# A two-layer attention and expert kernel on one core: the stores of the scan's values, and the seam between the layers

## The chip, the core and the metric

The kernel runs on one core of one Trainium2 chip. The core has five engines which run side by side, each through its own list of instructions, in order: PE (TensorE: matrix products and transposes, with PEld for its weight loads), DVE (VectorE), ACT (ScalarE), POOL (GpSimd) and SP (SyncE, which here does nothing but issue transfers). Transfers (DMAs) run on 16 shared DMA engines; ScalarE and SyncE issue theirs to hardware queues, GpSimd to a software queue. Engines and transfers wait for each other through semaphores. In the profile, "ACTq", "SPq" or "POOLq" stands for an engine's transfer queue.

The metric is the device time of one execution, in microseconds (us). The time of a kernel is the median over several runs.

## What is computed

Two layers, each `x = x + attention(layernorm(x)) + experts(layernorm(x))`, on x of 8 batches x 512 tokens x 256 features, in 32-bit floats.

```python
x = L0_attn_x
xn = _layernorm(x, axis=-1)
x = x + _L0_attn_ref(xn, ...) + _L0_ffn_ref(xn, ...)
xn = _layernorm(x, axis=-1)
x = x + _L1_attn_ref(xn, ...) + _L1_ffn_ref(xn, ...)
```

Layer 0's attention is a recurrence over the tokens, forwards and backwards. Tokens are mixed with their neighbours in five ways; products of these give r, k, v, a gate g and a decay w; then for each of 16 heads (16 x 16 states)

```python
def fwd_step(S, inp):
    rt, kt, vt, wt = inp
    S = jnp.exp(wt)[..., None] * S + kt[..., None] * vt[..., None, :]
...
y = (y_f + y_b).transpose(1, 0, 2, 3).reshape(B, T, D)
y = y * jax.nn.sigmoid(dx @ gate_w + gate_b)
yn = ((yg - mu) / jnp.sqrt(var + eps)).reshape(B, T, D) * ln_w + ln_b
return yn * g @ Wo
```

Layer 0's experts: 8 of them, each token goes to the best two. Layer 1's attention is a sum of two: a causal one whose keys and values come through a 64-wide latent, and one with a window of 64 tokens, both with 16 query heads over 4 key and value heads, with rotary positions and normalised queries and keys. Layer 1's experts: 16 small ones in 4 groups (4 per token, from the best two groups), and a shared one that every token passes.

## The kernel before

**Storage order.** Layer 0 runs batch after batch. The normalised tokens of all batches lie in eight tiles, held0 to held7, until they have been stored, and layer 1 uses these places again. Work tiles of layer 0 come from a pool `rw`: tiles with the same tag share a place, so a new one waits until the old one's readers are done.

**Who sets the order.** The program is written as coroutines. A class `Turns` goes round the running ones and lets each put out instructions up to its next `yield`; a second list, `behind`, gets its turn after the first. So the order of instructions on PE, VectorE, ScalarE and SyncE is that of the turns; GpSimd's alone is put in order by the scheduler. [...]

**One batch of layer 0**, in the code's names:
- `projections(b)` (lines 740 to 910), for the batch after the one being scanned. `mixed` multiplies on PE (L764, tile m), mixes on VectorE (L770) and lets GpSimd add the tokens with an accumulating transfer (L774). `values` computes v, copies it to the tile v (L828) and stores it to `vd` in memory (L830, from ScalarE's queue), then k. `decays` makes the decay, r and the tiles dq and dqs (L885 to L896) and the gate g (L906).
- `spread(b, c, vg)` (L912 to L919) loads `vd` back with 8 transfers of 64 KB from SyncE (L917), each value spread over partitions, into one of four kv tiles.
- `scans` (L926 to L982): 128 steps, 16 for each batch. A step is, on VectorE, a product (L943), two scans along the tokens (L952 forwards, L960 backwards) and a product (L965), about 7 us in all; PE sums the heads (L971, tile ys). The loads for a step are issued ahead.
- `ending(b, c, y, z, x)` (L984 to L1049), twice a batch: gate (L990), normalise (L994 to L1028), times g on GpSimd (L1030, tile z). After the second half, PE multiplies with the output weights (L1040, tile o), ScalarE copies the result to the tile x (L1045), GpSimd adds the layer's input with an accumulating transfer (L1046), and after eight turns SyncE stores x to `after` (L1049).
- beside it the experts (L594 to L682): for each of 39 chunks GpSimd gathers the weights (wgu and wdn, L582) and the tokens' rows (xs, L592) by indirect transfers; PE transposes and multiplies (g and u L630, y L670); ScalarE and VectorE make h (L654, L639); ys is copied (L679) and stored to `outs` (L680).

**The seam.** `begin()` (L1062 to L1093) runs late in layer 0. ScalarE issues loads of layer 1's first constants (cstr, rtw, cbias, L1069 to L1071) and, when the last value has been spread, of weights (gq, go, lqkv at L1088, the shared expert's w1 at L1092). It also starts layer 1's entry and routing for batch 0. `entry(b)` (L285 to L328) loads `after` (L290), gathers the two expert outputs of each token on GpSimd (L299, tile y0), accumulates them on VectorE (L310), normalises (statistics L236, root on GpSimd L229, L243), transposes on PE (L269) and copies to the tile xT (L324). `routing(b)` (L330 to L384) chooses the experts, on VectorE mostly.

Layer 1 then loads its remaining constants (cst1, gdown, gup, lo_w, L1116 to L1127). Its first instructions on batch 0 are the squares sq_g and the scaled tokens xg_g (L1189, L1191), the latent product lat_g (L1197), the products qkv (L1215, L1219), rotation and normalising (L1237 to L1264) and the transposes of queries qT_g (L269); beside them runs the shared expert (g and u L1427, h L1464 to L1472, y L1483). The entries and routings of batches 1 to 7 stand in the list behind (L1505 to L1510).

## Time and profile before

| what | value |
|---|---|
| median of 3 runs | 2606.01 us (2602.91 to 2608.89) |
| the profiled execution's own time | 2599.81 us |
| its span, first to last instruction | 2598.0 us |
| mean clock granted to PE, as a share of full speed | 0.942 |
| last batch's o in layer 0 ends / first xg_g of layer 1 starts | 1401.3 us / 1413.1 us |

The profiled execution is 1.8 us longer than its span, and 6.2 us below the median. Busy times by stretch, where the bounds of the first rows are the 17th, 33rd and so on of the scan's first products (L943), one batch each:

| stretch, us | length | PE busy | VectorE busy | granted clock |
|---|---|---|---|---|
| 284.8 to 449.0 | 164.2 | 144.6 | 141.6 | 0.95 |
| 449.0 to 601.6 | 152.6 | 141.7 | 142.7 | 0.97 |
| 601.6 to 755.9 | 154.3 | 144.9 | 143.0 | 0.96 |
| 755.9 to 920.6 | 164.7 | 145.5 | 141.8 | 0.96 |
| 920.6 to 1072.9 | 152.3 | 141.6 | 142.8 | 0.96 |
| 1072.9 to 1229.9 | 157.0 | 145.4 | 142.9 | 0.93 |
| 1229.9 to 1413.0 | 183.1 | 104.0 | 141.9 | 0.74 |
| 1413.0 to 1560.0 | 147.0 | 123.8 | 92.7 | 0.94 |

How the views are read. The page's second part cuts the span into 40 slices of 65 us and gives the busy tenths of each engine. In the view of waits a line has the engine, the waiting instruction, after the arrow what released it, and then the sum of the waits in us, their number and the longest. In the timeline a line has the start and the busy time in us, the engine, the code line, the operation, what it writes and reads, and in brackets the idle time just before it and what ended it.

### The profile page before, as it was taken

To read this page: it belongs to the slowest core of one execution; us is meant where nothing else is said; L and a number is where in the kernel's file an instruction comes from. 1 tells how busy PE (TensorE), PEld (TensorE's weight loads), DVE (VectorE), ACT (ScalarE), POOL (GpSimd) and SP (SyncE) were. 2 spreads that over 40 slices of the span, in tenths; PEclk is the share of its full clock that TensorE was granted. 3 is DMA by queue.
4 is the path that set the end of the run, shared out by engine and by line. 5 is a ranking of instruction groups with operands and counts; after the bars stand their busy time and mean duration, and the time that the engine had idled before them with its cause. 6 is when DMAs were issued, how large, how long until landed. Compare 5 with 4: busy or idle time off the path is not lost. (4 is left out here: it accounts for less than half of the span.)

```text
span 2598.0 us, 32354 instructions
## 1 busy us (share of the span) xinstructions
PE 2301.5 (89%) x11772; PEld 1369.8 (53%) x11772; DVE 2027.3 (78%) x2695; ACT 973.9 (37%) x1794; POOL 484.4 (19%) x424
## 2 busy tenths in 40 slices
PE   6688898989988899899925799999999999999998
PEld 4265555656655566555602444554555555555555
DVE  6699979999897998989984656686767667685566
ACT  1334224343322434224202244444444444445444
POOL 1123332233332322333111110010101010000000
PEclk9779999999999999999956899999999999999999
DMA  7546676776766767675543100020111101000000
GB/s 234 137 116 179 159 188 169 183 199 170 198 181 156 185 176 201 188 173 172 152 119 104 47 21 26 9 60 15 37 30 29 38 21 38 17 26 17 21 1 26
DMA packets 113885, 274.01 MB, mean 105 GB/s; under 512 B 25760, under 2 KB 51136, under 8 KB 108608
## 3 DMA queue, kind: packets, MB, share of 16 engines
q0 software_dynamic: 38448, 145.12, 21.3%
q1 hardware_dynamic: 66304, 109.13, 15.6%
q10 hardware_dynamic: 8976, 17.70, 2.0%
q8 instruction: 95, 1.56, 0.3%
q14 instruction: 62, 0.51, 0.1%
HBM read 215.22 MB, written 31.46 MB: 95 GB/s over the span
## 5 line engine op out<-in xcount | busy, mean ns | idle before, releaser
L670 PE MATMUL y<-wdn,h 128*128 128x256 f32 x936 | 271.5, 425 | 45.6 <-DVE h L639 38.3
L952 DVE TENSOR_TENSOR_SCAN kv<-dqs,kv 128x1024 f32<-128x1024 f32 x128 | 293.1, 2290 | 3.8
L960 DVE TENSOR_TENSOR_SCAN kv<-ds,kv 128x1024 f32<-128x1024 f32 x128 | 292.0, 2281 | 1.8
L670 PEld LDWEIGHTS y<-wdn,h 128*128 128x128 f32 x936 | 174.2, 203 | 165.2 <-issue 76.0
L630 PE MATMUL g<-xsT,wgu 128*128 128x256 f32 x936 | 227.5, 386 | 0.0
L1333 ACT ACTIVATE pt_g<-sc_g 128x512 f32<-128x512 f32 (+1 forms) x384 | 170.9, 533 | 148.7 <-PE sc_g L1325 140.9
L1483 PE MATMUL y<-w,h 128*128 128x256 f32 x768 | 202.9, 402 | 5.6 <-DVE h L1472 4.8
L630 PEld LDWEIGHTS g<-xsT,wgu 128*128 128x128 f32 x936 | 175.8, 192 | 53.5 <-issue 30.0
L1427 PE MATMUL g<-xT,w 128*128 128x512 f32 x384 | 192.4, 624 | 8.9 <-DVE h L1469 4.1
L630 PE MATMUL u<-xsT,wgu 128*128 128x256 f32 x780 | 196.5, 392 | 2.0 <-ACT h L654 2.0
L943 DVE TENSOR_TENSOR kv<-kv,k 128x1024 f32<-128x1024 f32 x128 | 159.3, 1244 | 45.1 <-DMA kv<-vd 45.0
L1427 PE MATMUL u<-xT,w 128*128 128x512 f32 x384 | 191.7, 621 | 1.8 <-DVE h L1469 0.9
L630 PEld LDWEIGHTS u<-xsT,wgu 128*128 128x128 f32 x780 | 147.2, 194 | 53.4 <-issue 17.3
L1483 PEld LDWEIGHTS y<-w,h 128*128 128x128 f32 x768 | 138.8, 193 | 62.6 <-issue 36.1
L965 DVE TENSOR_TENSOR kv<-kv,r 128x1024 f32<-128x1024 f32 x128 | 156.4, 1222 | 3.1
L971 PE MATMUL ys<-kv,cst 128*32 128x512 f32 x512 | 103.2, 659 | 60.8 <-DVE kv L965 60.8
L654 ACT ACTIVATE h<-g 128x512 f32<-128x512 f32 (+1 forms) x117 | 60.9, 525 | 234.2 <-PE g L630 222.8
L1333 ACT ACTIVATE pt_l<-sc_l 128x384 f32<-128x384 f32 (+1 forms) x256 | 98.2, 472 | 123.0 <-PE sc_l L1325 82.7
L592 POOL DMA_INDIRECT xs<-normed,whose x78 | 123.0, 1577 | 49.3 <-issue 18.0
L1470 DVE TENSOR_TENSOR h<-h,u 128x512 f32<-128x512 f32 x96 | 66.0, 687 | 76.2 <-PE u L1427 71.8
L1341 DVE TENSOR_TENSOR pt_l<-pt_l,cst 128x768 f32<-128x768 f32 (+1 forms) x128 | 108.0, 885 | 18.1 <-ACT pt_l L1333 18.1
L582 POOL DMA_INDIRECT wgu<-in_w_gu,wrow x39 | 66.4, 1703 | 287.4 <-PE u L630 285.7
(313 smaller groups left out, 3820.0 us busy)
## 6 DMA issues: line engine op xcount, KB each, us to landing
kv<-vd SPq DMA_DIRECT2D x1024, 64.0 KB
xf<-xnT POOLq DMA_DIRECT2D x40, 512.0 KB
cb<-cd SPq DMA_DIRECT2D x128, 128.0 KB
outs<-ys POOLq DMA_DIRECT2D x39, 256.0 KB
w<-in_w ACTq DMA_DIRECT2D x12, 384.0 KB
xn<-in_x SPq DMA_DIRECT2D x8, 512.0 KB
xnT<-xT ACTq DMA_DIRECT2D x16, 256.0 KB
normed<-xn SPq DMA_DIRECT2D x8, 512.0 KB
```

What stands on the lines that cost most here:

```text
L592: pool_e.indirect_dma_start(out=xs[:, n, :], out_offset=None, in_=normed, in_offset=bass.IndirectOffsetOnAxis(ap=whose[:, at : at + 1], ax ...
L630: pe.matmul(o, w[:, at + c * P : at + (c + 1) * P], xT[:, c, :], start=c == 0, stop=c == NC - 1,)
L670: pe.matmul(y[:, n, :], hs[j // 2][lo:, j % 2, n * P : (n + 1) * P], wd[lo:, j * D : (j + 1) * D], start=j == 0, stop=j == NJ0,)
L943: vec_e.tensor_tensor(kv, kv, bc(kc, 1, NV), ALU.mult)
L952: vec_e.tensor_tensor_scan(out=flat, data0=qc, data1=flat, initial=0.0, op0=ALU.mult, op1=ALU.add)
L960: vec_e.tensor_tensor_scan(out=flat[:, ::-1], data0=dc[:, ::-1], data1=flat[:, ::-1], initial=0.0, op0=ALU.mult, op1=ALU.add,)
L965: vec_e.tensor_tensor(kv, kv, bc(rc, 1, NV), ALU.mult)
L971: pe.matmul(y[r0 : r0 + 32, :], C["take"][:, 24 - 8 * at : 56 - 8 * at], kv[:, i, :], start=at == 0, stop=at == 3, skip_group_check=True,)
L1333: act_e.activation(pt[:, i, :end], scs[i][:, :end], AF.Exp, scale=0.25)
L1341: vec_e.tensor_tensor(pt[:, :, a0 : a0 + m], pt[:, :, a0 : a0 + m], bc(mask[:, :m], 1, 4), ALU.mult,)
L1427: pe.matmul(ps, w[:, k, c * P : (c + 1) * P], xT[:, c, :], start=c == 0, stop=c == NC - 1,)
L1483: pe.matmul(y[:, i, :], hs[k][:, (t + i) * P : (t + i + 1) * P], w1[j - 5 + k][:, 2, :], start=k == 0, stop=k == 5,)
```

## The change

Five things are changed.

1. The store of v to `vd` goes out from ScalarE's queue for the first batch alone, from GpSimd's for the other seven.
2. The tag "x" is gone. Two tiles of the routing of layer 0 (past, parts) and the tile x of batches 0 to 6 take the tag "dq" (one place); x is taken at the end of `ending`.
3. For the last batch, x is the tile held5. SyncE loads the layer's input into it ahead, and VectorE adds o to it straight from PSUM, in place of ScalarE's copy, GpSimd's accumulating load and the eight turns.
4. The constants cst1 are loaded in `begin()`, behind cstr, and gdown and gup behind lqkv.
5. `entry(1)` runs in layer 0, after the routing of batch 0; the list behind in layer 1 starts at batch 2. The routing of batch 1 stays in that list.

```diff
@@ two_layers
+    cst1 = const.tile([P, NCONST - last1], F32, name="cst1")
@@
-            past = tmp([P, NCH, E0], "past", "x")
+            past = tmp([P, NCH, E0], "past", "dq")
...
-            parts = rw.tile([P, 5, NTT], F32, tag="x", name="parts")
+            parts = rw.tile([P, 5, NTT], F32, tag="dq", name="parts")
@@ values
-                act_e.dma_start(vd.rearrange("(c p) t -> p c t", p=P), v)
+                (act_e if first else pool_e).dma_start(vd.rearrange("(c p) t -> p c t", p=P), v)
@@ scans
-                    x = rw.tile([P, NT, D], F32, tag="x", name=f"x_{b}")
...
-                        turns.add(ending(b, c, y, z, x))
+                        turns.add(ending(b, c, y, z))
@@ ending
             made.pop(b)
+            final = b + 1 == B
+            if final:
+                x = held(5, [P, NT, D], f"x_{b}")
+                nc.sync.dma_start(x, tokens(a["x"][b]))
+            else:
+                x = rw.tile([P, NT, D], F32, tag="dq", name=f"x_{b}")
             yield
...
-                act_e.copy(x[:, t : t + 2, :], ps)
-            pool_e.dma_start(x, tokens(a["x"][b]), accum_op=ALU.add)
-            for _ in range(8):
-                yield
+                if final:
+                    vec_e.tensor_tensor(x[:, t : t + 2, :], x[:, t : t + 2, :], ps, ALU.add)
+                else:
+                    act_e.copy(x[:, t : t + 2, :], ps)
+            if not final:
+                pool_e.dma_start(x, tokens(a["x"][b]), accum_op=ALU.add)
+                for _ in range(8):
+                    yield
             nc.sync.dma_start(tokens(after[b]), x)
@@ begin
             act_e.dma_start(cstr, a["cst"][:, first1:last1])
+            act_e.dma_start(cst1, a["cst"][:, last1:])
+            for n, (lo, hi) in _C.items():
+                if lo >= last1:
+                    C[n] = cst1[:, lo - last1 : hi - last1]
...
-            turns.add(then(entry(0), routing(0)))
+            turns.add(then(entry(0), routing(0), entry(1)))
...
-                ("lqkv", "l_wqkv", [P, NC, D + P]),
+                ("lqkv", "l_wqkv", [P, NC, D + P]), ("gdown", "g_kv_down", [P, NC, 64]),
+                ("gup", "g_up", [64, P]),
@@ layer 1
-        cst1 = keep.tile([P, NCONST - last1], F32, name="cst1")
-        act_e.dma_start(cst1, a["cst"][:, last1:])
...
-        gdown = keep.tile([P, NC, 64], F32, name="gdown")
-        act_e.dma_start(gdown, a["g_kv_down"])
-        gup = keep.tile([64, P], F32, name="gup")
-        act_e.dma_start(gup, a["g_up"])
+        gdown, gup = W["gdown"], W["gup"]
...
-                for b in range(1, B)
+                for b in range(2, B)
```

More of the change, by code (lines that the diff above doesn't have):

```diff
@@ L965, in scans, with sums @@
                 vec_e.tensor_tensor(kv, kv, bc(rc, 1, NV), ALU.mult)
-                def sums(b=b, c=c, vg=vg, kv=kv, y=y, z=z, x=x):
+                def sums(b=b, c=c, vg=vg, kv=kv, y=y, z=z):
                     for i in range(NV):
@@ L982, in scans, with ending @@
                 sums()
-        def ending(b, c, y, z, x):
+        def ending(b, c, y, z):
             sig, g = made[b]["sig"], made[b]["g"]
@@ L1114, in two_layers @@
         ps_o = l1.enter_context(tc.tile_pool(name="ps_o", bufs=1, space=PSUM))
-        cst1 = keep.tile([P, NCONST - last1], F32, name="cst1")
-        act_e.dma_start(cst1, a["cst"][:, last1:])
-        for n, (lo, hi) in _C.items():
-            if lo >= last1:
-                C[n] = cst1[:, lo - last1 : hi - last1]
         gq, go, lqkv = W["gq"], W["go"], W["lqkv"]
-        gdown = keep.tile([P, NC, 64], F32, name="gdown")
-        act_e.dma_start(gdown, a["g_kv_down"])
-        gup = keep.tile([64, P], F32, name="gup")
-        act_e.dma_start(gup, a["g_up"])
+        gdown, gup = W["gdown"], W["gup"]
         lo_w = keep.tile([P, NC, D], F32, name="lo_w")
```

## The prediction

> **What bounds the kernel now.** I read the page first: its busy shares and 40 slices, the waits of each engine's instructions, then the timeline of two places.

> ```profile
> PE 2301.5 (89%) x11772; PEld 1369.8 (53%) x11772; DVE 2027.3 (78%) x2695; ACT 973.9 (37%) x1794; POOL 484.4 (19%) x424
> ...
> PE   6688898989988899899925799999999999999998
> ...
> DVE  6699979999897998989984656686767667685566
> ...
> PEclk9779999999999999999956899999999999999999
> ```

> One slice is 65 us. Layer 0 ends near 1402 us (slice 21), layer 1 starts at 1413. From slice 25 PE is full, so layer 1 is PE's; in layer 0 PE and VectorE are both near 90%, in a fixed order with each other, and at slices 20 to 22 neither is: that is the junction, with PE's clock down.

> ```profile
> SPq L917 <- DMA vd<-v: 122.4, 8, 36.9
> ...
> SPq L917 <- DMA cstr<-in_cst: 11.9, 1, 11.9
> ...
> DVE kv L943 <- DMA kv<-vd: 45.0, 10, 9.3
> ...
> DVE xg_g L1191 <- DMA after<-x: 20.8, 1, 20.8
> PE lat_g L1197 <- DVE xg_g L1191: 11.5, 1, 11.5
> PE qT_g L269 <- DVE qn_g L1259: 7.6, 1, 7.6
> ```

> SyncE's queue, which loads the scan's values (L917), waits 8 times for a store `vd<-v`. One batch of layer 0 shows why that is odd:

> ```profile
> 352.75 0.37 ACTq L830 DMA_DIRECT2D vd<-v  x1
> 357.81 4.53 SPq L917 DMA_DIRECT2D kv<-vd  x9
> 362.25 1.23 DVE L943 TENSOR_TENSOR kv<-kv,k 128x1024 f32<-128x1024 f32 x1 [6.56 <-DMA kv<-vd]
> ```

> At 357.81 SyncE loads the scan's 8th step of a batch. It needs that batch's vd, stored 150 us before; yet it goes only when the next batch's vd, issued at 352.75 from ScalarE's queue, has landed. That is a wait for an order of completions among the hardware queues, not for data, and VectorE stands idle 6.56 us at L943. It comes once for each of the stores b = 1 to 7.

> **Part 1, the stores b >= 1 go to GpSimd's queue.** The stalls at L943 which follow a vd store are, at 200.47, 362.25, 670.21, 833.76 and 1143.77 us, 3.55, 6.56, 6.84, 6.59 and 8.94 us; at the other two stores (511.61, 983.17) nothing is left of it. Sum 32.5 us. The two last stalls of the row, 1.57 at 1310.69 and 9.31 at 1334.70, follow the constant loads in begin() (cstr and others), not vd; they stay. What one stall is worth depends on what comes next, since VectorE's lead lasts only until it waits for PE:
> - b = 1: nearly whole, 3.5 us.
> - b = 2: PE is busy through the stall, and VectorE's mixing (L770, at 368.65) waits for PE's m of 365.25. With the lead it would start at 366.5 and no earlier: about 1.8 us. b = 5 has the same order and numbers: 1.8 us.
> - b = 4: PE waits 2.33 us for L770 at 676.92 and then runs slowly, m in 2.73 us instead of 1.13 and u in 3.78 instead of 1.88. Without the stall the gate L990, at 686.53, would come at about 681.4: 5.1 us.
> - b = 7: L990 at 1160.54 would come at about 1152.8, as m was ready from 1143: 7.7 us.

> Sum 3.5 + 1.8 + 5.1 + 1.8 + 7.7 = 19.9, say 20 us. Check by batch periods: from scan step to scan step the batches last 164.2, 152.6, 154.3, 164.6, 152.3 and 157.0 us; the two without a stall are the short ones, and those with the stalls of b = 2, 4, 5 and 7 exceed 152.5 by 11.7, 1.8, 12.1 and 4.5. Their sum, 30, is near the stalls' 28.9, but batch by batch they don't match my leads, and PE's work in them is some 3 us larger (144.6 to 145.5 against 141.6), so I don't price by periods. Bounds: 0 if PE takes every lead, 32.5 if none is lost.

> Cost on GpSimd: the nearest row is its 512 KB accumulate (L1046), 1.29 to 1.45 us each, so 7 x 1.4 = 10 us on an engine that is 19% busy. Behind the stores stand gathers: for b = 2 the down weights, which were issued at 355.06 (they waited for PE y till 354.80) and are used at 373.63, 18.6 us later; for b = 1, 4, 7 one row gather of xs, used 27 us later; for b = 3 and 6 GpSimd is idle some 14 us there (504.12 to 518.46). Cost taken: 0; without that cover up to 10 us. The new true wait, the next batch's first load after its store, has some 75 us of slack, and SyncE's later loads stand behind it.

> The slow m and u belong to PE's clock: granted 0.58 at 676 to 683 us after a wait of 2.33, 0.72 at 207 to 213 after one of 2.41. [...]

> **Part 2, the junction.** Before, the last batch's tokens go through ScalarE's copy, GpSimd's accumulating load, the store and then layer 1's first reads:

> ```profile
> 1401.33 0.58 ACT L1045 COPY x<-o 128x512 f32<-128x512 f32 x1 [2.08 <-PE o L1040]
> ...
> 1402.21 1.43 POOL L1046 DMA_DIRECT2D x<-in_x  x1 [6.29 <-ACT x L1045]
> ...
> 1409.95 0.38 SPq L1049 DMA_DIRECT2D after<-x  x1
> ...
> 1413.10 0.88 DVE L1191 TENSOR_SCALAR xg_g<-xT,vecs 128x512 f32<-128x512 f32 x2 [20.84 <-DMA after<-x]
> 1413.64 3.67 PE L1197 MATMUL lat_g<-xg_g,gdown 128*64 128x512 f32 x4 [11.49 <-DVE xg_g L1191]
> ```

> From the load's issue to the store's is 7.7 us, to lat_g 11.5. After, VectorE adds o to tokens that lie ready: 2 adds of about 0.7 us (like the 128x512 adds of L990, 0.69), and 2 copies, the load and its landing fall away. But entry(1) now stands in front of them: the accesses of one engine keep their order, and VectorE's 8 accumulations (L310), the statistics and the normalising (L243) of batch 1 come before and between the adds; PE's second half of o waits for the first add (one PSUM bank), and then come batch 1's transposes, one g and one u of the shared expert and the router, and only then lat_g. In times of before:
> - GpSimd waits 23.95 us for ScalarE ahead of z (L1030), which ends at 1395.9. The last four of entry(1)'s gathers stand behind it: 1.27 us apart, the last issued at 1400.0, landing 2.8 us after (as 1425.97 to 1428.77 in before's entry(1)).
> - last accumulation to 1403.3, statistics 2.2, first add 0.7: 1406.4; normalising to 1408.5; o's second half beside it; transposes to 1410.8; xT's copies, g, router and u to 1417.9 (at the slow clock); lat_g to 1419.9, where before it ended at 1417.3. So at this point the change is 2.6 us later.
> - What it wins comes behind: in before entry(1) and routing(1) (some 13.6 us of VectorE) lay between lat_g and the heads' chain; VectorE is 9.3 us of 10 busy from 1450 on, with PE idle 12.4 us of 25, 7.6 of them ahead of qT_g at 1471.3. Now routing(1) stands ahead of the ropes, which start at 1441.5 (before 1443.5) and run without it: last norm about 1456, qT_g at 1456.5 where it was 1471.3: 14.8 us. PE allows it: it has 39.7 us of work from 1413.64 to 1471.3, less 3.0 moved up, plus 0.6 for the slow clock: 1455 at the earliest.

> From 1475 PE never waits long (92 to 97% per 100 us), so the lead is kept to the end. Taken: 14 us; bounds: 17 (all idle time of PE in 1413 to 1475, 18 us, less one) and 3 (the ropes wait for something else and only the 2.6 us against 5.6 of early idle are played out).

> **Part 3, the rest.** The constants move to begin(): two small loads (gdown, gup) and cst1, three more DMAs of 0.34 to 0.48 us each (rows 1401.34 to 1402.20) on ScalarE's queue, and as many fewer at the junction, where ScalarE has 11 us of idle time. SyncE's kv loads wait on these by the same order of completions (11.9 us for cstr, 8.1 for go); cst1 stands now among them. I take 0, bounds +3 (one more wait like the 2.0 for lqkv) and -2. The `x` tile's users go to the dq tile: x is stored 40 us before dq is written again (last landing 362.5, next write 408.9): 0.

> **Sum.** 20 + 14 + 0 = 34 us. The profiled run is 2599.81 (span 2598.0 and 1.8 around it): span 2564, run 2566. The median, 2606.0, lies 6.2 higher; I carry the difference over: 2572.

> **Rivals.**
> - B, PE takes layer 0's leads. For: PE is 141.6 to 145.5 us busy in each batch of 152 to 165, no less than VectorE, so what VectorE wins PE might only wait out; b = 2 shows it. Against: the batches without a stall are shorter by 12. Only the junction is left: 2606 - 14 = 2592.
> - C, the junction gives nothing. For: lat_g now ends a chain from GpSimd's gathers to the router, with PE near half clock; if one landing takes as long as the accumulate's 7.7 us rather than 2.8, 5 us go, and if the ropes still wait for constants or routing, the other 10 do. Against: 7.6 us at qT_g are measured. Time 2606 - 20 = 2586.
> - D, the change doesn't do what it says: the kv loads are late because of traffic (172 GB/s in the long batches) and not because of the store's completion. Against: SyncE's release coincides with the landing to 0.01 us at 357.81. Then the junction alone is left, 2592, or with C nothing, 2606.
> - E, slower: the stores hold GpSimd. A store that stands in its queue until landed, 7.7 us as L1046's chain, makes the gathers behind it late; if their cover (18.6 us ahead of the down weights, 27 for xs) were used up already, PE would wait 7 x 7.7 = 54 us for y or xsT: 2606 - 34 + 54 = 2626. It decides from 34 / 7 = 4.9 us for each store on. Against: 1.29 us was measured at 500.28 beside a running scan, and the cover is measured too. [...]

> **Chances.** My forecast, both parts, 0.55; B 0.15; C 0.16; D 0.05 (half of it at 2592, half at 2606); E 0.04; neither part worth anything, 0.05, at 2606. A measurement can tell 0.2%, 5.2 us, from no change. Faster 0.55 + 0.15 + 0.16 + 0.025 = 0.885; same 0.05 + 0.025 = 0.075; slower 0.04. Range: low end 2606 - 32.5 - 17 - 2 = 2554; the upper end takes in C and B, each with some 5 us about it: 2598. Outside are 0.115 above and a little of the forecast below.

> **What would show it.** Right: SyncE's waits have `vd<-v` once or not at all and L943's list loses five entries, with the two of begin() still there; the batches between scan steps that had the stalls of b = 2, 4, 5 and 7 last 162.4, 149.2, 162.8 and 149.3 us; VectorE's 20.8 us at xg_g and PE's 7.6 us at qT_g are gone, while lat_g starts some 4 us later against o's first half. Wrong: unchanged batch periods with no L943 stall (B); PE idle before lat_g longer than 15 us (C); stalls still there behind other releasers (D); idle time of PE y or xsT behind gathers, with GpSimd spans at vd above 5 us (E).

## The result and the profile after

| kernel | median of the runs, us | lowest to highest | profiled span, us |
|---|---|---|---|
| before | 2604.46 (4 runs) | 2599.08 to 2608.89 | 2598.0 |
| changed | 2561.09 (4 runs) | 2558.75 to 2563.55 | 2559.0 |

The ratio is 0.9829, with a 95% interval from 0.9810 to 0.9849: the change takes 43 us away. The forecast was 2572 us, with a range from 2554 to 2598; the medians' gain was put at 34 us and is 43. The two profiled executions differ by 39.0 us, because the one of before was a short one among its runs. What follows accounts for these 39.

The page of the changed kernel, its busy times and its 40 slices (64 us each):

```profile
PE 2296.1 (90%) x11772; PEld 1366.0 (53%) x11772; DVE 2028.2 (79%) x2697; ACT 971.8 (38%) x1792; POOL 477.1 (19%) x430
...
PE   6789899999989899899835999989899999999998
...
DVE  6599979999997998999986666675867577675566
...
PEclk9769898999999999999956999999999999999999
```

Each engine does the work it did before: PE is busy for 2296 us against 2301, VectorE for 2028 against 2027. Nearly all that went is idle time; PE's 5 us less go with its clock, which was granted at half for 302 us in the trace of before and for 287 in that of the changed kernel. The hole at the seam (PE 2, 5, 7 before) is now 3 and 5, and PE is full one slice earlier.

Waits of the changed kernel (engine, waiting instruction, what released it; us in total, number, longest):

```profile
SPq L918 <- DMA kv<-vd: 95.1, 90, 4.6
...
SPq L918 <- DMA vd<-v: 40.2, 1, 40.2
```

```profile
PE o L1046 <- DVE x L1052: 7.3, 1, 7.3
```

```profile
DVE kv L943 <- DMA kv<-vd: 12.4, 4, 7.2
...
PE qT_g L270 <- DVE qn_g L1266: 2.3, 1, 2.3
```

SyncE waits for a store of vd once, where it waited 8 times; the one that is left is the first batch's, whose values it truly needs. VectorE's waits at L943 fell from 45.0 us in 10 to 12.4 in 4, and the longest of these, 7.2, belongs to begin(). The idle times ahead of xg_g (20.8 us, VectorE) and lat_g (11.5, PE) are gone; a new one stands ahead of the second half of o (L1046), 7.3 us, and the one ahead of qT_g fell from 7.6 to 2.3.

The timeline at the second batch's store, which the prediction showed for before:

```profile
334.55 22.81 SPq L918 DMA_DIRECT2D kv<-vd  x24
...
352.89 0.76 POOL L831 DMA_DIRECT2D vd<-v  x1 [3.47 <-ACT v L829]
355.49 1.22 DVE L943 TENSOR_TENSOR kv<-kv,k 128x1024 f32<-128x1024 f32 x1
```

SyncE issues the same 24 loads in 22.8 us where it took 27.7, and the product of the 24th scan step starts without waiting, 6.8 us earlier. GpSimd needs 0.76 us to issue the store.

The seam in the changed kernel:

```profile
1374.22 1.25 POOL L1030 TENSOR_TENSOR z<-z,g 128x512 f32<-128x512 f32 x1 [18.83 <-ACT z L1028]
...
1378.43 0.48 DVE L311 SCALAR_TENSOR_TENSOR acc<-y,wslot,acc 128x256 f32<-128x256 f32 x1 [4.78 <-DMA y<-outs,slot]
...
1385.02 0.69 DVE L1052 TENSOR_TENSOR x<-x,o 128x512 f32<-128x512 f32 x1
...
1385.76 3.78 PE L1046 MATMUL o<-wmix,z 128*128 128x256 f32 x8 [7.30 <-DVE x L1052]
...
1397.12 1.93 PE L1204 MATMUL lat_g<-xg_g,gdown 128*64 128x512 f32 x4
...
1433.27 1.09 PE L270 MATMUL qT_g<-cst,qn_g 128*128 128x128 f32 x8 [2.31 <-DVE qn_g L1266]
```

It runs as it was worked out: the last gathers wait for z, VectorE for the gathers, o's first add for VectorE, and lat_g comes behind batch 1's transposes. Layer 0 ends 20.46 us earlier than in before (from the 125th scan step to the last batch's z the two run in parallel). lat_g at 1397.12 is thus 3.9 us later against that than it was; qT_g at 1433.27 is 17.6 us earlier.

If the same instructions are compared step by step, the lead of the changed kernel over before goes like this:

| up to | lead, us | gained on the way | forecast |
|---|---|---|---|
| first product of the scans | -3.44 | -3.4 | 0 |
| 17th scan step (stall of b = 1) | 0.61 | 4.1 | 3.5 |
| 33rd (b = 2) | 2.35 | 1.7 | 1.8 |
| 49th (b = 3) | 2.80 | 0.5 | 0 |
| 65th (b = 4) | 8.34 | 5.5 | 5.1 |
| 81st (b = 5) | 10.39 | 2.1 | 1.8 |
| 97th (b = 6) | 10.23 | -0.2 | 0 |
| 113th (b = 7) | 18.59 | 8.4 | 7.7 |
| 125th (begin()) | 20.46 | 1.9 | 0 |
| first transposes of keys, kT_g | 40.64 | 20.2 | 14 |
| layer 1, from 2040 us of before to 2550 | 38.5 | -2.1 | 0 |
| last instruction | 39.0 | 0.6 | 0 |

The five batches with a stall gained 21.8 us, all seven together 22.0.

One execution is a small sample, and the table sets one of the changed kernel against one of before. Nine profiles of this study have the stores on GpSimd and four kv tiles. In these the gains are 2.9 to 7.3 us up to the 17th step, 0.9 to 2.2 for b = 2, 4.9 to 6.0 for b = 4, 1.3 to 4.4 for b = 5 and 7.9 to 8.7 for b = 7, in all 20.4 to 25.4 up to the 113th step. Of the first piece and of b = 5 the table thus shows the order of size and no more.

### The profile page after: what moved, and what is told of

The parts are those of the page before. It is cut to its first block, busy times and chain, and to the rows that moved or that the text cites. A ratio compares the mean times of both kernels' runs of the same rounds, so it can differ in the third digit from the quotient of the medians.

```text
span 2559.0 us, 32385 instructions
## 1 busy us (share of the span) xinstructions
PE 2296.1 (90%) x11772; PEld 1366.0 (53%) x11772; DVE 2028.2 (79%) x2697; ACT 971.8 (38%) x1792; POOL 477.1 (19%) x430
## 3 DMA queue, kind: packets, MB, share of 16 engines
q0 software_dynamic: 38928, 148.26, 21.8%
q8 instruction: 95, 1.56, 0.3%
## 5 line engine op out<-in xcount | busy, mean ns | idle before, releaser
L1340 ACT ACTIVATE pt_g<-sc_g 128x512 f32<-128x512 f32 (+1 forms) x384 | 170.9, 532 | 149.4 <-PE sc_g L1332 141.6
L943 DVE TENSOR_TENSOR kv<-kv,k 128x1024 f32<-128x1024 f32 x128 | 162.4, 1269 | 12.5 <-DMA kv<-vd 12.4
L971 PE MATMUL ys<-kv,cst 128*32 128x512 f32 x512 | 109.5, 670 | 57.4 <-DVE kv L965 44.8
L1348 DVE TENSOR_TENSOR pt_l<-pt_l,cst 128x768 f32<-128x768 f32 (+1 forms) x128 | 108.0, 885 | 18.1 <-ACT pt_l L1340 18.1
L1348 DVE TENSOR_TENSOR pt_g<-pt_g,cst 128x512 f32<-128x512 f32 x128 | 85.1, 685 | 39.5 <-ACT pt_g L1340 39.4
```

The source lines that it names most:

```text
L943: vec_e.tensor_tensor(kv, kv, bc(kc, 1, NV), ALU.mult)
L971: pe.matmul(y[r0 : r0 + 32, :], C["take"][:, 24 - 8 * at : 56 - 8 * at], kv[:, i, :], start=at == 0, stop=at == 3, skip_group_check=True,)
L1340: act_e.activation(pt[:, i, :end], scs[i][:, :end], AF.Exp, scale=0.25)
L1348: vec_e.tensor_tensor(pt[:, :, a0 : a0 + m], pt[:, :, a0 : a0 + m], bc(mask[:, :m], 1, 4), ALU.mult,)
```

## The experiments

Each was timed against before on the same chip. Three chips were used, and the medians of before on them were 2607.8, 2608.1 and 2604.7 us.

**One part alone: the store.**

```diff
-                act_e.dma_start(vd.rearrange("(c p) t -> p c t", p=P), v)
+                (act_e if first else pool_e).dma_start(vd.rearrange("(c p) t -> p c t", p=P), v)
```

> The kernel before with one edit: the stores of v for b >= 1 go from GpSimd's queue. Theory (the stalls at L943 come from the order of completions among the hardware queues; the leads are kept): 2604 - 22 = about 2582 us, five stalls at L943 gone, lead at the 113th scan step about 22 us, and it stays to the end. Rival 1 (the leads are worth something only with the new seam): 2595 to 2604, the lead gone by the first product of layer 1. Rival 2 (the stores cost GpSimd's gathers something): the stalls gone but idle time of PE y or xsT up, 2590 or more.

2585.62 us, ratio 0.9918 (0.9892 to 0.9944): 22 us. Its waits at L943 for loads are

```profile
DVE kv L943 <- DMA kv<-vd: 6.0, 4, 2.4
```

The five stalls behind stores are gone; begin()'s long one is still there (9.4 us at the 125th step, which the list puts under another name). At the 113th scan step the lead over before is 21.55 us, 23.4 from the first product on, and at the first kT_g it is 22.7. The first rival, which has it gone there, is wrong; so is the second, as the gathers cost no time in layer 0. But 6.4 us of the lead are lost later in layer 1 of this execution, so that 16.3 are left at its end, and in that the theory failed (see "Loss not forecast" below). The medians have the full 22.

**The other part alone: the seam.**

```diff
-                (act_e if first else pool_e).dma_start(vd.rearrange("(c p) t -> p c t", p=P), v)
+                act_e.dma_start(vd.rearrange("(c p) t -> p c t", p=P), v)
```

> The changed kernel with the store of v back on ScalarE's queue for all batches: held tile, constants and entry(1) early are kept. Theory (two independent parts): 2604 - 20 = about 2584 us, all stalls of before at L943 back, qT_g some 17 us earlier against the end of the scans. Rival (part of the seam's 20 us came because layer 0 ended in another state): 2590 to 2594.

2586.65 us, ratio 0.9920 (0.9898 to 0.9941): 21 us. Its waits at L943:

```profile
DVE kv L943 <- DMA kv<-vd: 37.0, 8, 9.0
```

The stalls are back, and with them in place this profile gains 20.1 us at the seam, as the changed kernel does with 20.2: how layer 0 ended does not show in it. The two parts' ratios multiply to 0.9839, inside the interval of both together, so nothing shows that one part needs the other.

**The seam without the early entry.**

```diff
-            turns.add(then(entry(0), routing(0), entry(1)))
+            turns.add(then(entry(0), routing(0)))
...
-                for b in range(2, B)
+                for b in range(1, B)
```

> The changed kernel with entry(1) back in layer 1's list behind. Theory A (held tile and early entry each fill one half of the hole): lat_g starts some 11 us earlier than in before against the end of the scans, but PE waits again ahead of qT_g; 2561 + 8 = about 2569 us. Theory B (the early entry alone makes the gain, since it takes VectorE's work out of the heads' chain): 2561 + 17 = about 2578 us.

2571.75 us, ratio 0.9869 (0.9846 to 0.9893). Its latent product and its wait ahead of qT_g:

```profile
1382.42 1.90 PE L1204 MATMUL lat_g<-xg_g,gdown 128*64 128x512 f32 x4 [0.37 <-PE u L1434]
```

```profile
PE qT_g L270 <- DVE qn_g L1266: 7.8, 1, 7.8
```

The end of its scans leads before's by 20.1 us, so lat_g comes 11.1 us earlier than there, as theory A has it, and PE waits 7.8 us ahead of qT_g again. Of the seam's gain 10.2 us are there, half. That is nearer to A (2569) than to B (2578).

**The seam without the held tile.**

```diff
-            final = b + 1 == B
+            final = False
```

> The changed kernel with the old end of the last batch (ScalarE's copy, GpSimd's accumulating load, eight turns, tile of tag dq), entry(1) early. Theory B (with the entry early, its chain of gathers, accumulations and transposes covers the old end's 7.7 us of load and the store): 2561 to 2564 us. Theory A (the held tile is worth its 11.5 us of PE's idle time also now): about 2572 us.

2565.79 us (2560.12 to 2572.41), ratio 0.9846 (0.9821 to 0.9872). By the medians it stands between the theories, but its runs vary by 12 us, and the profiled one has the same lead as the changed kernel: 19.95 us gained at the seam against 20.2. Its timeline:

```profile
1383.05 1.44 POOL L1056 DMA_DIRECT2D x<-in_x  x1 [3.46 <-ACT x L1054]
1389.06 0.38 SPq L1059 DMA_DIRECT2D after<-x  x1
1392.10 1.07 DVE L1198 TENSOR_SCALAR xg_g<-xT,vecs 128x512 f32<-128x512 f32 x2 [5.05 <-DMA after<-x]
1396.67 1.50 PE L1204 MATMUL lat_g<-xg_g,gdown 128*64 128x512 f32 x3
```

The old chain of copy, load and store is there, and xg_g waits 5 us for it; lat_g comes no later, since batch 1's transposes and the shared expert stand ahead of it on PE anyway. With the entry early, the profile shows no worth of the held tile, and the medians, 5 us apart, leave it open; without the early entry it is worth 10 us. So the early entry fills the hole from both ends.

**Is it the order, or the traffic?** First by loading further ahead, with the store on ScalarE:

```diff
-            kv = rw.tile([P, NV, T], F32, tag="kv", name=f"kv{c}{vg}_{b}", bufs=4)
+            kv = rw.tile([P, NV, T], F32, tag="kv", name=f"kv{c}{vg}_{b}", bufs=5)
...
-                if n + 1 < len(todo) and ("keys", todo[n + 1][0]) in done:
-                    kvs[todo[n + 1]] = spread(*todo[n + 1])
+                for s in todo[n + 1 : n + 3]:
+                    if s not in kvs and ("keys", s[0]) in done:
+                        kvs[s] = spread(*s)
```

> The changed kernel with all stores of v back on ScalarE's queue, but a fifth kv tile and the scan's values loaded two steps ahead (cst1 is loaded at the seam again, to make room). Theory (a load waits only for the order of completions, some 5 us of landing): the wait falls on a load that is needed a step, about 10 us, later, the stalls of 3.5 to 9 us at L943 are gone with the store still on ScalarE, and the time is that of the changed kernel or lower, 2550 to 2563 us. Rival (the store's traffic, or the transfers' own duration, makes the values late): the stalls stay and it is near the kernel with the seam alone, 2585 us.

2576.00 us, ratio 0.9871 (0.9849 to 0.9893). A miss: neither value. The stall of b = 1 is gone, those of b = 2, 4, 5 and 7 are as before:

```profile
334.72 31.42 SPq L917 DMA_DIRECT2D kv<-vd  x24
...
352.80 0.37 ACTq L830 DMA_DIRECT2D vd<-v  x1
362.33 1.23 DVE L942 TENSOR_TENSOR kv<-kv,k 128x1024 f32<-128x1024 f32 x1 [6.59 <-DMA kv<-vd]
```

SyncE starts its run of 24 loads where it did in before (334.68): PE's sums release the tiles two steps at a time, and a fifth tile did not move this run. In the program's list of waits the load that waits for the store is still that of the same step for b = 2, 4, 5 and 7, and a step later for b = 1, the one whose stall is gone. The remedy failed, and what it says of the theory is one case out of five.

So the store itself was moved, still on ScalarE's queue, behind the products of k:

```diff
-                (act_e if first else pool_e).dma_start(vd.rearrange("(c p) t -> p c t", p=P), v)
                 yield
 
                 k, pss = yield from projected(xk, 1, "k")
+                act_e.dma_start(vd.rearrange("(c p) t -> p c t", p=P), v)
```

> The changed kernel with the store of v on ScalarE's queue again, but put out after the products of k instead of before them. In the program's order of completions the load that waits for it is then that of the 25th and the 73rd scan step for b = 2 and 5 (a step later than before), and still that of the 8th, 56th and 104th for b = 1, 4 and 7. Theory (the wait is for the order of completions): the stalls near 362 and 834 us are gone, since those loads are needed some 10 us later, and the other three stay and grow by the store's delay; 2561 + 4 + 5.5 + 8.4 = about 2579 us, or a little more. Rival (the store's traffic or a hardware queue as such delays the loads): all five stalls stay, about 2585 us.

2577.67 us, ratio 0.9898 (0.9874 to 0.9922), with 2579 expected. The store of b = 4 and the step that it holds up, and then that of b = 2:

```profile
662.39 0.37 ACTq L834 DMA_DIRECT2D vd<-v  x1
667.83 5.08 SPq L918 DMA_DIRECT2D kv<-vd  x8
670.41 1.23 DVE L943 TENSOR_TENSOR kv<-kv,k 128x1024 f32<-128x1024 f32 x1 [6.53 <-DMA kv<-vd]
```

```profile
359.42 1.22 DVE L943 TENSOR_TENSOR kv<-kv,k 128x1024 f32<-128x1024 f32 x1
360.61 0.37 ACTq L834 DMA_DIRECT2D vd<-v  x1
```

With the same bytes on the same queue, the stalls of b = 2 and 5 went, the two whose store now stands behind the step's load in the order of completions. Those of b = 1, 4 and 7 stayed (3.69, 6.53 and 8.88 us); they did not grow as expected. At the 41st and 89th steps small ones came (1.41 and 1.61). These are the two that the order of completions had named in advance. By itself it leaves something to the traffic, since for b = 2 and 5 the loads of the step are now out before the store. Two other facts leave it nothing: in this trace the store of 360.61 counts on semaphore 100, and SyncE's next load on 100, at 367.44, is the one that waits for it; and in the changed kernel the same bytes, stored by GpSimd at the same time (352.89 for 352.75), hold up no load. The wait is for the order.

**Does a store cost GpSimd anything?** Each of the seven was issued twice, the second time to memory that nobody reads.

```diff
+                if not first:
+                    vd2 = dram.tile([D, T], F32, tag="vd2", name=f"vd2_{b}")
+                    pool_e.dma_start(vd2.rearrange("(c p) t -> p c t", p=P), v)
```

> The changed kernel with each of the seven stores of v issued twice from GpSimd, the second time to a place that nobody reads. Theory (a store costs GpSimd 1.4 us that other work covers): 2561 us, within 2. Rival (the stores hold up the gathers behind them): 7 x 1.4 = 10 us to 7 x 7.7 = 54 us more, 2571 to 2615 us.

2562.40 us (2560.96 to 2563.31), ratio 0.9823 (0.9805 to 0.9840): nothing that can be told from the changed kernel. Seven more stores, 0.72 to 0.79 us each, beside running scans, are covered.

**The stalls that are left,** by moving begin()'s loads (cstr, cst1, rtw, cbias, the weights) to GpSimd:

```diff
-            act_e.dma_start(cstr, a["cst"][:, first1:last1])
+            pool_e.dma_start(cstr, a["cst"][:, first1:last1])
...
-                act_e.dma_start(w1[j], a["w1"][j])
+                pool_e.dma_start(w1[j], a["w1"][j])
```

> The changed kernel with all loads of begin() issued from GpSimd's queue instead of ScalarE's. Theory (the two stalls left at L943, 2.1 and 7.2 us, wait for the completions of these loads in the hardware queues): they go, and as VectorE alone bounds the end of layer 0 the 9 us are kept: 2561 - 9 = about 2552 us. Rival (the loads stand ahead of entry(0)'s and entry(1)'s gathers on GpSimd and the seam starts later): 2560 us or more, with L943's stalls gone and VectorE idle at the accumulations.

2556.64 us (2555.30 to 2562.29), ratio 0.9807 (0.9786 to 0.9829). The waits at L943 are

```profile
DVE kv L943 <- DMA kv<-vd: 2.6, 2, 2.0
```

and between the 113th and the 125th step it gains 9.1 us on the changed kernel (1.9 at the 123rd step, 7.3 at the 125th), of which 6.4 are left at the last instruction. The medians differ by 4 us only (2561.09 and, in another group of runs, 2556.64); this profiled execution also reached its first scan product 5.25 us later than the changed kernel's did (see the last section). So the stalls go, as the theory has it, but not all of the 9 us is kept. On one chip, added to the edit of the gathers (below), the same edit takes 8 us off the median.

The same stalls, by loading ahead (the edit of the fifth tile, with the stores on GpSimd):

> The changed kernel (stores on GpSimd) with a fifth kv tile and loads two steps ahead, cst1 loaded at the seam. Theory (all stalls left at L943 are waits of one step's length): 7.2 + 2.1 at begin(), some 2 to 3 elsewhere, so 2561 - 10 = about 2551 us. Rival (SyncE's loads wait for PE's sums to free the tiles, not for the order, and come no earlier): 2561 us, stalls as before.

2559.58 us (2555.28 to 2568.68), ratio 0.9825 (0.9799 to 0.9852). The stalls at begin() are still there, 1.2, 6.4 and 1.7 us at the 123rd, 125th and 126th steps, so for these the rival is right, for the reason seen above. The two small ones that the changed kernel has elsewhere (1.8 and 1.6 us, at the 27th and 75th) are gone.

**The wait that the change brought,** PE's 7.3 us ahead of o's second half. entry(1)'s gathers went into tiles that are free sooner:

```diff
-                y = temp([P, 2, 2, D], "y0", f"y0_{b}_{t}", ahead // 2)
+                y = temp([P, 2, 2, D], "y1" if b == 1 else "y0", f"y0_{b}_{t}", ahead // 2)
...
-                "y0": ("xf", 2), "gt4": ("t5a", 1), "eq4": ("th", 1), "gt16": ("dx", 1),
+                "y0": ("xf", 2), "y1": ("v", 2), "gt4": ("t5a", 1), "eq4": ("th", 1), "gt16": ("dx", 1),
```

> The changed kernel with entry(1)'s gathers put into the two tiles of tag v, which are free by then, so that GpSimd issues all eight before the last batch's z and not four of them behind it. Theory (at the seam PE waits 7.3 us for the first add of o, which VectorE does only after the last gathers' accumulation and statistics): accumulation done at 1375.6 instead of 1382.7, lat_g about 7 us earlier, and the lead kept: 2561 - 7 = about 2554 us. Rival (VectorE, with routing(1) and the shared expert, is the bound behind lat_g): the lead is lost by qT_g, 2559 to 2561 us.

2556.26 us (2551.30 to 2559.43), ratio 0.9806 (0.9786 to 0.9826). Its timeline:

```profile
1378.10 4.75 DVE L311 SCALAR_TENSOR_TENSOR acc<-y,wslot,acc 128x256 f32<-128x256 f32 x8
...
1385.11 0.69 DVE L1052 TENSOR_TENSOR x<-x,o 128x512 f32<-128x512 f32 x1
...
1385.85 1.99 PE L1046 MATMUL o<-wmix,z 128*128 128x256 f32 x8 [0.81 <-DVE x L1052]
```

The eight accumulations run without a wait, PE's 7.3 us are 0.81, and o's second half takes 1.99 us for its 8 products, where the changed kernel took 3.78 at a granted clock of 0.50. Against the 125th scan step lat_g and qT_g both come 8.4 us earlier than in the changed kernel; 7.5 are left at the end. The lead is kept.

**Both together.**

> The edit of e10_gathers together with that of e6_begin_pool (begin()'s loads from GpSimd's queue). Theory (two separate places): 2561 - 9 - 7 = about 2546 us. Rival (the two share a cover, the wait for the last batch's z): only the larger, 2552 to 2554 us.

2548.33 us (2543.39 to 2554.49), ratio 0.9781 (0.9758 to 0.9803). It is the fastest kernel here: 56 us below before, and 11 below the changed kernel on the same chip. That lies between the theory and the rival. From the 113th to the 125th step the profile gains 11.0 us, as with begin()'s loads alone; but up to the first kT_g the seam then gives 25.3, where the gathers alone give 28.6 and the changed kernel 20.2, so 5.1 of the gathers' 8.4 us are left. One loss can be seen: o's second half takes 3.78 us again, as in the changed kernel.

**The changed kernel again,** beside the three above.

> The changed kernel as it is, on the same chip as the others of this call. 2561 us, ratio to the kernel before 0.983; the first product of the scans shows how much its start (111.4 us in the profile of the changed kernel, 108.0 in that of before) differs from run to run.

2559.61 us (2557.25 to 2565.33), ratio 0.9825 (0.9804 to 0.9847): the result repeats. The gain of the gathers alone over it, 3 us by the medians, is not beyond the spread of the runs, and rests on the profiles; that of both together, 11 us, is.

## Why the prediction was right, and where it was off

- **The mechanism of the stalls** was right: the wait is for an order of completions and not for data (the semaphores and the store moved behind k show it), and D falls.
- **What a stall is worth** was right batch by batch: 1.8 forecast and 1.7 measured for b = 2, with a stall of 6.56; 5.1 and 5.5 for b = 4; 7.7 and 8.4 for b = 7, and these three come again in the other profiles. The sum is 21.8 for 19.9. For b = 1, 4.1 for 3.5 is partly luck, as this piece varies from 2.9 to 7.3. To follow VectorE's lead to where it next waits for PE was the right way; the sum of the stalls, 32.5, would have been half as much again. By the batch periods they would have come out wrong one by one, as the text had it: that of b = 2 and that of b = 4 fell to 162.5 and 148.8 us, where 162.4 and 149.2 were forecast.
- **B falls** with the store alone (22 us), **C** with the seam alone (21 us), **E** with the doubled store. The forecast put 1.4 us on a store by the accumulating loads; it is 0.76.
- **PE's slow clock in b = 4** is gone with the wait, as the sum had it. In before the products m (L764) that wait behind the stall start at 676.92 and take 2.73 us; in the changed kernel the same ones start at 671.70 and take 1.13. The windows of 7 us about it are, before first (length; PE, PEld, VectorE, ScalarE, GpSimd busy with counts; then PE's granted clock, the DMA share and GB/s):

```profile
676.00:683.00 7.00, 6.08 (x12) 3.63 (x13) 6.65 (x8) 0.00 (x0) 2.52 (x2) 0.58 0.99 241
```

```profile
671.00:678.00 7.00, 7.00 (x35) 4.30 (x34) 6.52 (x7) 1.19 (x2) 2.52 (x2) 1.00 0.72 197
```

In before the wait of 2.33 us ahead of that m ends at 676.92, and the clock is recorded at half from 677.12 to 683.95, 6.83 us; in the changed kernel there is no such wait, and the clock is full from 585.1 to 718.2. The other experiments bear out the wait: the lists of PE's waits have m behind the mixing where the stall of b = 4 stands (before 11.4 us in 5 waits, the seam alone 11.8 in 5, the fifth tile with the store on ScalarE 8.3 in 4, the store behind k 8.8 in 3), and in eight profiles with the stores on GpSimd not at all.

- **The seam** was the term that was mis-sized: 14 us forecast, 20.2 measured. lat_g was put at 1417.9 in times of before and came at 1417.6. The chain up to there was right step by step, but for two small errors that cancel: batch 1's transposes ended 0.7 us later than put, and the products behind them ran at full clock (recorded so from 1390.7 on) and not at the slow one.

  The step that failed is the next: the rotations (ropes) at 1441.5, qT_g at 1456.5, and "PE allows it ... 1455 at the earliest". In times of before the ropes came at 1439.3 and qT_g at 1453.7, 17.6 us earlier than in before and not 14.8. VectorE set that time, as PE still waited 2.3 us for the norm; PE itself would have been ready at 1451.4. The bound of 1455 had taken PE's work at before's durations, and these held slow stretches behind before's own waits: by waits of 2.77 us (to 1436.66), 4.80 (to 1458.77) and 7.57 (to 1471.30) the clock was at half for 3.41 us from 1438.29, 3.41 from 1458.77 and 6.83 from 1469.01. From 1438.3 to 1475.8 the granted clock was 0.82 in before, and products y took up to 0.63 us each; in the changed kernel they take 0.38, and the clock is 1.00 from 1391 to 1518. Why the ropes came 2.2 us sooner than put is not shown, and the prediction gives no terms for its 1441.5.

  From qT_g to kT_g another 2.6 us were gained, and there the terms are seen: the eight qT_g take 1.09 us in place of 1.97, the six y 1.56 in place of 2.34, and cT, 1.02 us in before, no longer stands between. These waits went, but for 2.3 us of the last, and the slow time with them. For b = 4 this was counted, here it was not.
- **The early entry is what makes the seam's gain.** The prediction described both edits as one chain. In the profiles the held tile alone gives 10 us, the early entry alone 20, and both together 20.
- **begin()'s two stalls** were put at no change and gave 1.9 us here. That is within their own spread: over the six profiles with these stores on GpSimd and begin() as in the changed kernel, the piece goes from -0.5 to 1.9.
- **Loss not forecast:** 2.1 us of the lead are given back in layer 1, between 1677 and 2040 us of before. Some 1.6 us lie in one place, where products g ran at half clock in the changed execution (1.06 us each for 0.59, from 1985.7 on). The rest was not followed up, and it can't be laid to the change: from the first kT_g to the last instruction before's one profile takes 1121.8 us and the other thirteen 1121.4 to 1128.2, the store alone being the longest.
- **In the profiles the total** came nearer than the parts by luck. The parts gained, 22.0 + 1.9 + 20.2 = 44.1 us, are 10 above the 34 of the sum, and in the 39.0 between the two profiles a start that was 3.4 us later and the loss in layer 1 hide half of that. The gain of the medians, 43, is near the parts.

## What to carry to other kernels

A stall behind a load is first to be asked what released the load's issue. Where that is a transfer that it doesn't need, on another engine's queue, moving the one transfer to another kind of queue was worth what VectorE's or PE's next wait left of each stall (here 21.8 us of 32.5), and that could be read batch by batch from the timeline. At a seam between two stages, work of the later stage that waits behind nothing should go into the hole, and then the tiles it needs must be free early; and where the trace shows a slow clock behind a wait of PE, as in b = 4 with 6.83 us at half the clock behind a wait of 2.33, it is to be counted with the wait.

## What the hardware showed that was not expected

The start of this kernel is not the same from one execution to the next. Up to the first scan product, which the changes don't touch, before needed 108.0 us and the changed kernel 111.4, and over the 14 profiles of this study the values go from 104.6 to 116.7, which is more than several of the gains looked for. From 82 to 92 us the two windows are, before first:

```profile
82.00:92.00 10.00, 10.00 (x34) 5.20 (x34) 3.13 (x10) 3.80 (x6) 0.40 (x1) 0.94 0.58 99
```

```profile
82.00:92.00 10.00, 10.00 (x27) 6.06 (x27) 3.17 (x10) 1.44 (x3) 0.45 (x1) 0.59 0.58 100
```

PE is busy through both, with a granted clock of 0.94 in one and 0.59 in the other; the same products r take 0.59 us in the first and 1.06 in the second, and that makes the 3.44 us by which the changed kernel came late. In before a stretch at half clock runs from 76.4 to 83.2 us, in the changed kernel from 76.5 to 90.2: 6.8 us more at half the clock, which is 3.4 us of work. So equal work lay at different clocks. In the clock records of these two traces the clock is either full or half; at half are 29 stretches in before and 24 in the changed kernel, and but for the last, which the program's end cuts off, they are from 3.41 to 88.75 us long in the one and from 3.41 to 102.40 in the other. Why a stretch begins where it does is not shown. The start's share of the differences between two profiles has to be taken off before they are compared, as was done above.

The stores from GpSimd beside VectorE's scans took 0.72 to 0.79 us each to issue, doubled or not, where 1.4 had been put, and the time did not move with seven stores more (2562.40 us for 2561.09).
